# A decoder layer on one core: a long convolution done by halves of the channels, beside the projections

## The chip, the core and the metric

The kernel runs on one core of one Trainium2 chip, in float32. The core has a matrix engine (TensorE, PE in the profile), a vector engine (VectorE, DVE), a scalar engine (ScalarE, ACT), a general engine (GpSimd, POOL), a queue engine that issues DMAs (SyncE, SP), and 16 DMA engines which every queue shares. TensorE writes its products to PSUM, which has eight banks of 128 x 512 float32; the other data lies in SBUF, in 128 partitions, or in DRAM. The metric is the time on the device in microseconds (us), the median of several executions of the same program.

## What is computed

One decoder layer over 16 sequences of 512 tokens and 256 channels: a long-convolution block with a gated MLP, an attention block over the sequence and a context, and a low-rank feed-forward block, each followed by a layer norm of the sum. The change lies in the first block, whose mixing part is this:

```python
z = rmsnorm(u, pre_norm_w) @ in_proj_w.T            # 256 -> 768 channels
z_pre = depthwise_conv(z, short_w, 3 taps) + short_b
x2, x1, v = split(z_pre, 3)                         # 256 channels each
h = sum(residues[:, :, None] * exp(log_poles * t), axis=1)   # 256 filters, 512 long
xv = x1 * v
yconv = causal_conv(xv, h)                          # by rfft in the reference
y = (yconv + xv * D_skip) * x2
y = y @ out_proj_w.T + u
```

x2 is called the gate in the kernel.

## The kernel before

**A planner.** Nearly all work is recorded as operations with an engine (or two to choose from), a guessed cost, a priority number, the buffers it reads and writes, and a latency for DMAs. `Plan.schedule` (L104) plays the operations through with these costs: whenever an engine is free, it takes the startable operation with the lowest priority number. Buffers come from pools of a fixed number of tiles, and an operation is startable only when a tile is free. The result is a fixed order of instructions on each engine. On the chip each engine goes through its own list strictly in order and waits at an instruction until its inputs are there; the costs have no further effect. On TensorE, `change` (L96) adds `HOLD` or subtracts `STAY` to the priority, so that operations which split the array in the same way stay together. There are two plans, one for the front (L376, emitted at L875) and one for everything after it (L928, emitted at L1672). The second plan's instructions follow the first's on every engine.

**The front: projections.** For each sequence `project` (L422) loads x into a tile of the pool "x" (L428, after the preparation of the sequence three earlier), takes the sums of squares on ScalarE (L317), the power on GpSimd (L306 and L307), scales each of four chunks of rows on VectorE (L330), and transposes on TensorE (L344) with copies to a second "x" tile, xT. Six projections of 128 channels follow (L456, each into one bank of PSUM), with the short convolution on each: one tap and the bias on ScalarE (L463), two taps on VectorE straight from PSUM (L471). Projections 0 and 1 are the gate, which goes to DRAM (`gates`, L481). Projections 2 and 4, and 3 and 5, are multiplied on GpSimd (L487) to x1 * v of the first and the second 128 channels, transposed (L495) and copied into `xv` (L299 or L297 by engine), one tile of 256 channels x (4 pieces x 16 sequences) with the position in a piece along the partitions.

**The front: the long convolution.** Each channel's sequence of 512 is cut into 4 pieces of 128. Within a piece the convolution is a product with a 128 x 128 Toeplitz matrix, which is loaded from DRAM (`hpad`, L593, 0.5 MB for eight channels, in a tile of "x") and cut to a triangle on GpSimd (L602). Between pieces the filter is a sum of 16 exponentials, so that states are enough: `near_mm` (L619) makes the states of the pieces, VectorE (L629) and GpSimd (L639, L647) chain them, and `far_mm` (L683) multiplies them by powers of the poles, which ScalarE makes (L655). `toe_mm` (L670) and `far_mm` add up in the same PSUM bank; a copy (L299 or L297) takes it out, and two stores on ScalarE's queue (L701) write it to `yconv` in DRAM. There are eight blocks of 32 channels. Every block needs `xv` of all sequences: an operation there reads the whole of `xv`, and so all blocks stand behind the last sequence's projections.

**Pools and order.** Pool "x" has 11 tiles, used by x, xT, the Toeplitz tiles and `far`; "row" has nine of 128 x 512; "mm" is the eight banks of PSUM. Five Toeplitz loads are allowed early, the others after the last sequence's preparation (L595). The main stage begins with `first_block` (L996), which loads `yconv` (L1002, two halves), the gate (L1008) and x (L1011) for one sequence, multiplies on GpSimd (L1020) and projects on TensorE (L1033). The tiles of the main stage lie where the front's tiles lay and wait for those to be released. At its beginning it also fills some constant tiles and stores four small ones in DRAM (L924).

Of the kernel before, what the change touches and what calls it, by code (L numbers as in the profile page):

```python
# [61 lines left out]
class Plan:  # L62
# [9 lines left out]
    def __init__(self, tiles):  # L72
        self.tiles, self.ops = tiles, []

# [18 lines left out]

    HOLD, STAY = 1000, 1000
# [104 lines left out]
def decoder_layer(  # L199
# [71 lines left out]
    gates = dram.tile([B, P, KD * T], F32, name="gates")  # L271
    weights = ctx.enter_context(tc.tile_pool(name="weights", bufs=1))
# [52 lines left out]
    def scale_ops(x, sq, prio, on="DVE"):  # L325
        for c in range(NT):

            def fn(e, c=c):
                if e == "DVE":
                    nc.vector.tensor_scalar(x.t[:, c, :], x.t[:, c, :], sq.t[:, c, 8:9], None, ALU.mult)  # L330
                else:
                    nc.scalar.activation(x.t[:, c, :], x.t[:, c, :], AF.Copy, scale=sq.t[:, c, 8:9])

            plan.op(on, 0.4 if on == "DVE" else act(D, True), fn, prio, r=[sq], w=[(x, c)])
# [24 lines left out]

    R8 = 8  # L360
    NR = D // HPG
    with ExitStack() as front:
        fp_ = front.enter_context(tc.tile_pool(name="front", bufs=1))
        fps = front.enter_context(tc.tile_pool(name="psf", bufs=1, space=PSUM))
        pool = {
            "mm": tiles(fps, "fmm", 8, [P, T]),
            "x": tiles(fp_, "fx", 11, [P, R8 * P]),
# [8 lines left out]
        plan = Plan(pool)  # L376
# [4 lines left out]

        xv = fp_.tile([P, D, NT * B], F32, name="xv")
# [29 lines left out]
        XV, HPAD, NEAR, INW, CW, LP, W = (Buf("none") for _ in range(7))  # L412
        pool["none"] = [None] * 7
        marks = []

        def at_seq(b):
            return marks[b : b + 1] if b >= 0 else ()

        def load_in(dst, src, prio, w, after=()):
            plan.op("SP", 0.4, lambda e: nc.sync.dma_start(out=dst, in_=src), prio, w=w, lat=4.0, after=after)  # L420

        def project(b):  # L422

            pr = b * 100
            x_ = View("x", lambda t: t.rearrange("p (c d) -> p c d", c=NT))
            plan.op(
                "SP", 0.4,
                lambda e: nc.sync.dma_start(out=x_.t, in_=x[b].rearrange("(c p) d -> p c d", p=P)), pr - 1000,  # L428
                w=[x_], lat=4.0, after=at_seq(b - 3),
# [17 lines left out]
            scale_ops(x_, sq, pr - 120)  # L447
            xT = transposed(x_, lambda t: t, pr - 120, View("x", lambda t: t.rearrange("p (k n) -> p k n", k=KD)))
            marks.append(plan.ops[-1])
            zs = {}  # L450
            for m in (2, 4, 3, 5, 0, 1):
                ps, t = Buf("mm"), Buf("row")

                def mm(e, m=m, ps=ps):
                    for k in range(KD):
                        nc.tensor.matmul(  # L456
                            ps.t, inw[:, k, bass.ts(m, P)], xT.t[:, k, :], start=(k == 0), stop=(k == KD - 1)
                        )

                plan.op("PE", KD * pe(T), mm, pr + 10, r=[xT, INW], w=[ps])  # L460
                plan.op(
                    "ACT", act(T, True),
                    lambda e, m=m, ps=ps, t=t: nc.scalar.activation(  # L463
                        t.t, ps.t, AF.Identity, bias=cb[:, m : m + 1], scale=cw[:, m, 2:3]
                    ),
                    pr + 10, r=[ps, CW], w=[t],
                )
                for lag in (1, 2):
                    plan.op(
                        "DVE", dve(T) + 0.05,  # L470
                        lambda e, m=m, lag=lag, ps=ps, t=t: nc.vector.scalar_tensor_tensor(  # L471
                            t.t[:, lag:], ps.t[:, 0 : T - lag], cw[:, m, 2 - lag : 3 - lag], t.t[:, lag:],
                            ALU.mult, ALU.add,
                        ),
                        pr + 10, r=[ps], w=[t],
                    )
                zs[m] = t
                if m < KD:
                    plan.op(
                        "SP", 0.4,  # L480
                        lambda e, m=m, t=t: nc.sync.dma_start(out=gates[b][:, bass.ts(m, T)], in_=t.t), pr,  # L481
                        r=[t], lat=3.0,
                    )
            for k in range(KD):
                plan.op(
                    "POOL", 1.3,
                    lambda e, a=zs[KD + k], c=zs[2 * KD + k]: nc.gpsimd.tensor_tensor(a.t, a.t, c.t, ALU.mult),  # L487
                    pr, r=[zs[2 * KD + k]], w=[zs[KD + k]],
                )
            for k in range(KD):  # L490
                ps = Buf("mm")

                def tr(e, k=k, ps=ps):
                    for j in range(NT):
                        nc.tensor.transpose(ps.t[:, bass.ts(j, P)], zs[KD + k].t[:, bass.ts(j, P)], ident)  # L495

                plan.op("PE", TR, tr, pr, r=[zs[KD + k]], w=[ps])
                plan.op(
                    "ACT DVE", (1.04, 1.04),
                    lambda e, k=k, ps=ps: copy(  # L500
                        e, xv[:, bass.ts(k, P), b :: B].rearrange("p d j -> p j d"),
                        ps.t.rearrange("p (j d) -> p j d", j=NT),
                    ),
                    pr, r=[ps], w=[(XV, (b, k))],
                )

        for b in range(B):
            project(b)

        for k, (dst, src) in enumerate(((lp, poles), (rs, resid))):  # L510
            load_in(dst[:, :, 0:NS], src, 100 + k, [(LP, k)], at_seq(0))
        load_in(sk, skip, 102, [(LP, 2)], at_seq(0))
        load_in(lprow.rearrange("(k p) n -> p k n", p=P), poles, 110, [(NEAR, "row")], at_seq(1))
# [68 lines left out]
        for blk in range(NR // R8):  # L582
            pc = 5000 + blk * 100
            d0 = blk * R8 * HPG
            toes = []
            for c in range(HPG):
                toe = View("x", lambda t: t.rearrange("p (d u) -> p d u", u=P))

                def load_toe(e, toe=toe, at=d0 + c * R8):
# [5 lines left out]
                early = blk * HPG + c < 5  # L595
                plan.op(
                    "SP", 0.4, load_toe, pc - 50, r=[HPAD], w=[toe], lat=4.0,
                    after=at_seq(4 + c if early else B - 1),
# [13 lines left out]
            far = View("x", lambda t: t.rearrange("p (r u) -> p r u", u=P))  # L612
            for rr in range(0, R8, 2):

                def near_mm(e, rr=rr, ps=ps, d0=d0):
                    for r in range(rr, rr + 2):
                        for c in range(HPG):
                            d = d0 + c * R8 + r
                            nc.tensor.matmul(  # L619
                                ps.t[bass.ts(c, SLOT), bass.ts(r, (NT - 1) * B)],  # L620
                                near[:, d * NS : d * NS + SLOT], xv[:, d, 0 : (NT - 1) * B],
                                start=True, stop=True,
                            )

                plan.op("PE", 0.25, near_mm, pc, r=[XV, NEAR], w=[ps], tiling=COLS4)
# [370 lines left out]
    def first_block(b, after):  # L996
# [16 lines left out]
        for k in range(KD):  # L1013
            plan.op("SP", 0.1, lambda e, k=k: load_y(e, k), p0 - 500, w=[(yt, k)], lat=4.0)
# [740 lines left out]
```

## Time and profile before

| | us |
|---|---|
| median of 3 runs | 2184.96 |
| lowest and highest | 2181.42, 2185.18 |
| the profiled execution, its own time | 2186.31 |
| its span, first to last instruction | 2184.6 |
| TensorE busy in the span | 2037.0 (93%) |
| VectorE busy | 1361.0 (62%) |
| ScalarE busy | 943.6 (43%) |
| GpSimd busy | 663.5 (30%) |
| mean clock granted to TensorE | 0.97 of full speed |

The profile is one execution. Its span runs from the first to the last instruction; the execution's own time is 1.7 us longer. A line of groups reads: line of the kernel, engine, operation, tile written <- tiles read, shapes, count; then busy us and mean ns of one; then how long the engine stood idle just before such instructions and which instruction released it. PEld is TensorE's loading of weights, which overlaps its matmuls. A busy share over the whole span is a mean over stages with different limits, so the pieces of the span are read one by one. These are the page's own slices, 54.6 us each:

```profile
PE   8999758979899999999999999999999999999676
DVE  7988311746565757575757575757575757575642
PEclk9999978989999999999999999999999999999888
DMA  5342582122222222222232313131313131212200
```

The first six slices are the front.

### The profile page before, as it was taken

The numbers are of one execution on the slowest core, as the hardware profiler recorded it, in microseconds if no ns is written. First come the engines' busy times: TensorE is split into PE (matmuls) and PEld (weight loads), VectorE is DVE, ScalarE is ACT, GpSimd is POOL, SyncE is SP. The second block draws the span as 40 slices with busy tenths as digits, with TensorE's granted clock in tenths as the row PEclk, the third lists the DMA queues.
The fourth block names the chain that finished last, engine by engine and source line by source line (L and its number), as shares of the span: only waits on it lengthen the run. The fifth ranks groups of instructions, "written<-read, shape, count | busy, mean of one in ns | idle before, by whom it ended". The sixth has DMA issues, their size and how long they took to land.

```text
span 2184.6 us, 35354 instructions
## 1 busy us (share of the span) xinstructions
PE 2037.0 (93%) x14324; PEld 1053.6 (48%) x14324; DVE 1361.0 (62%) x1988; ACT 943.6 (43%) x1385; POOL 663.5 (30%) x896
## 2 busy tenths in 40 slices
PE   8999758979899999999999999999999999999676
PEld 4444545535454545454545454545454545454332
DVE  7988311746565757575757575757575757575642
ACT  7765312142526262626262626262626262625243
POOL 3333451131323232324232424242424242323222
PEclk9999978989999999999999999999999999999888
DMA  5342582122222222222232313131313131212200
GB/s 176 123 133 83 198 270 73 49 63 66 70 59 89 59 88 61 83 66 86 62 91 57 94 55 93 56 94 55 95 54 96 52 87 52 68 51 68 61 11 10
DMA packets 113733, 177.94 MB, mean 81 GB/s; under 512 B 13217, under 2 KB 61858, under 8 KB 113442
## 3 DMA queue, kind: packets, MB, share of 16 engines
q1 hardware_dynamic: 108450, 167.29, 25.0%
q10 hardware_dynamic: 5120, 8.39, 1.2%
q8 instruction: 112, 1.84, 0.3%
q14 instruction: 51, 0.42, 0.1%
HBM read 109.00 MB, written 66.67 MB: 80 GB/s over the span
## 4 chain that ended last, share of the span: by engine, by line
PE 84%; ACT 5%; DVE 5%; DMA 3%; issue 2%; POOL 1%; ACTq 0%; SPq 0%; POOLq 0%; DVEq 0%
PE mm L1058 13%; PE scores L1302 10%; PE mm L1211 8%; PE mm L1110 7%; PE scores L1380 7%; PE av L1415 7%; PE fmm L456 6%; PE mm L1605 4%; PE av L1621 3%; PE mm L1139 3%; PE mm L972 2%; DMA fx<-hpad 2%; PE mm L344 2%; PE mm L1467 2%; ACT ex L1392 2%
## 5 line engine op out<-in xcount | busy, mean ns | idle before, releaser
L1392 ACT ACTIVATE ex<-scores 128x2048 f32<-128x2048 f32 x160 | 300.1, 1876 | 176.7 <-PE scores L1380 174.0
L1058 PE MATMUL mm<-xT,w_l 128*128 128x512 f32 x640 | 296.0, 606 | 0.0
L1403 POOL TENSOR_SCALAR_AFFINE_SELECT ex<-ex 128x512 f32<-128x512 f32 x256 | 158.0, 635 | 382.4 <-ACT ex L1392 351.1
L1302 PE MATMUL scores<-keys,q 32*128 32x320 f32 (+4 forms) x2560 | 233.8, 472 | 42.8 <-DVE maxes L1332 18.3
L1321 DVE TENSOR_TENSOR scores<-scores,mask_qk 128x512 f32<-128x512 f32 (+1 forms) x192 | 168.3, 876 | 101.9 <-PE scores L1302 97.9
L1302 PEld LDWEIGHTS scores<-keys,q 32*128 32x128 f32 x2560 | 116.5, 190 | 179.0 <-issue 57.8
L1613 ACT ACTIVATE row<-mm,b_s 128x512 f32<-128x512 f32 x128 | 80.8, 684 | 253.6 <-PE mm L1605 253.4
L1380 PE MATMUL scores<-q,keys 32*128 32x512 f32 (+3 forms) x2048 | 183.1, 460 | 7.1 <-ACT ex L1392 7.0
L1058 PEld LDWEIGHTS mm<-xT,w_l 128*128 128x128 f32 x640 | 115.6, 190 | 145.9 <-issue 128.6
L456 PE MATMUL fmm<-fx,inw 128*128 128x512 f32 x384 | 177.2, 607 | 2.2 <-ACT fx L299 2.2
L957 ACT ACTIVATE xt<-xt,small 128x256 f32<-128x256 f32 x192 | 102.7, 595 | 173.7 <-POOL small L950 173.7
L1549 POOL TENSOR_TENSOR nd<-nd,nd 128x1024 f32<-128x1024 f32 x30 | 70.6, 2354 | 347.3 <-DMA nd<-di 347.3
L1415 PE MATMUL av<-ex,va 128*32 128x512 f32 (+3 forms) x2048 | 168.1, 439 | 0.0
L306 POOL TENSOR_SCALAR small<-small 128x4 f32<-128x4 f32 (+1 forms) x66 | 13.1, 199 | 509.6 <-DVE small L942 508.1
L1070 ACT ACTIVATE row<-mm 128x512 f32<-128x512 f32 x80 | 47.8, 597 | 271.0 <-PE mm L1058 271.0
L297 DVE COPY row<-av 128x512 f32<-128x512 f32 x66 | 45.7, 692 | 184.0 <-PE av L1415 165.5
L1110 PE MATMUL mm<-w_l,gT 128*128 128x256 f32 x640 | 158.9, 384 | 0.0
L471 DVE SCALAR_TENSOR_TENSOR frow<-fmm,cw,frow 128x511 f32<-128x511 f32 x192 | 140.2, 745 | 14.5 <-ACT frow L463 10.5
L1334 DVE TENSOR_REDUCE maxes<-scores 128x4 f32<-128x2048 f32 x64 | 146.7, 2293 | 2.2
L1380 PEld LDWEIGHTS scores<-q,keys 32*128 32x128 f32 x2048 | 89.3, 183 | 104.4 <-ACT ex L1392 33.8
L1110 PEld LDWEIGHTS mm<-w_l,gT 128*128 128x128 f32 x640 | 117.9, 190 | 43.8 <-issue 30.3
L1217 DVE TENSOR_SCALAR q<-mm,bqc_s 128x512 f32<-128x512 f32 x63 | 47.3, 751 | 140.0 <-PE mm L1211 140.0
(177 smaller groups left out, 3322.8 us busy)
## 6 DMA issues: line engine op xcount, KB each, us to landing
dn<-row SPq DMA_DIRECT2D x120, 256.0 KB
fx<-hpad SPq DMA_DIRECT2D x32, 512.0 KB
keys<-dk SPq DMA_DIRECT2D x64, 256.0 KB
nd<-dn SPq DMA_DIRECT2D x30, 512.0 KB
nd<-di SPq DMA_DIRECT2D x30, 512.0 KB
fx<-in_x SPq DMA_DIRECT2D x16, 512.0 KB
gates<-frow SPq DMA_DIRECT2D x32, 256.0 KB
yconv<-frow ACTq DMA_DIRECT2D x64, 128.0 KB
```

The source lines that it names most:

```text
L456: nc.tensor.matmul(ps.t, inw[:, k, bass.ts(m, P)], xT.t[:, k, :], start=(k == 0), stop=(k == KD - 1))
L471: lambda e, m=m, lag=lag, ps=ps, t=t: nc.vector.scalar_tensor_tensor(t.t[:, lag:], ps.t[:, 0 : T - lag], cw[:, m, 2 - lag : 3 - lag], t.t[ ...
L1058: nc.tensor.matmul(ps.t, w[:, k, bass.ts(f, P)], zT.t[:, k, :], start=(k == 0), stop=(k == KD - 1))
L1110: nc.tensor.matmul(ps.t[:, bass.ts(cc, D)], gT.t[:, f, bass.ts(c, P)] if f < NF else gE.t, w_l3[:, f, :] if f < NF else w_l3e[:, c, :], st ...
L1211: nc.tensor.matmul(ps.t, w[:, k, cols], xT.t[:, k, :], start=(k == 0), stop=(k == KD - 1))
L1302: nc.tensor.matmul(sc.t[:, r, at : at + hi - lo], q.t[hd, bass.ts(i, P)], kk.t[hd, lo:hi], start=True, stop=True,)
L1321: nc.vector.tensor_tensor(diag, diag, mask, ALU.add)
L1334: nc.vector.tensor_reduce(own[:, 3], sc.t, AX.X, ALU.max, negate=True)
L1380: nc.tensor.matmul(sc.t[:, r, at : at + T - j * P], keys[g].t[hd, TC + j * P : TC + (j + 1) * P], qas[g].t[hd, j * P :], start=True, stop= ...
L1392: lambda e, sc=sc, ex=ex: nc.scalar.activation(ex.t.rearrange("p (r n) -> p r n", r=HPG), sc.t, AF.Exp, scale=scale),
L1403: lambda e, ex=ex, at=at: nc.gpsimd.affine_select(out=ex.t.rearrange("p (r n) -> p r n", r=HPG)[:, :, at : at + P], in_=ex.t.rearrange("p ...
L1415: nc.tensor.matmul(av[g].t[bass.ts(r, SLOT), j * P :], va.t[:, j, h * VS : h * VS + SLOT], ex.t[:, r * T + at : r * T + at + n], start=(j ...
```

## The change

The convolution is done by halves of the channels. `xv` becomes two tiles, one for each 128 channels, with a dependency of its own, so that the first four blocks need only the first half of x1 * v. The loop over sequences is split: `prepare` makes xT, `x1v(b, k, ...)` makes one half of x1 * v for a sequence, `gate_of` makes its gate. The first seven sequences do all of it as before. The last nine (`LATE`) do only the first half of x1 * v in this pass; their second halves and gates follow with higher priority numbers (3000 and up), between the operations of the first half's convolution (2000 to 2310). The last two gates (`LAST`) have 7000, behind the second half's convolution (5400 and up). The xT of the last five sequences (`KEPT`) stays in its tile until then. Four others are written to a new array in DRAM, `normed`, and read back.

Beside that:

- The scaling of rows in the front moves from VectorE to GpSimd (`scale_ops(..., "POOL")`).
- The `yconv` stores move from ScalarE's queue to SP, with a planned cost of 0.6.
- `far` gets a tile of its own, one, and "x" has 10 tiles in place of 11.
- `near_mm` of a block is one operation in place of four, `far_mm` one in place of two, with its two halves of the array taken in turn.
- A projection holds its "row" tile from the matmul on, and near_mm its "state" tile.
- The planned costs of DMAs on SP follow their size (`MB` = 3.5 us for 1 MB), and the planned latencies are changed.
- In the front's plan `HOLD` is 0 in place of 1000. The main plan keeps 1000 and 1000.
- In `first_block` x and the gate are loaded ahead of `yconv`, with a planned cost of 0.5 in place of 0.1.
- Three Toeplitz loads are allowed early, after the preparations 13 to 15; the second half's after the second-half x1 * v of the sixth late sequence.

The diff, cut to its core:

```diff
-                if e == "DVE":
-                    nc.vector.tensor_scalar(x.t[:, c, :], x.t[:, c, :], sq.t[:, c, 8:9], None, ALU.mult)
+                if e == "POOL":
+                    nc.gpsimd.tensor_scalar(x.t[:, c, :], x.t[:, c, :], sq.t[:, c, 8:9], None, ALU.mult)
...
+        xv = [fp_.tile([P, P, NT * B], F32, name=f"xv{k}") for k in range(KD)]
...
-            "x": tiles(fp_, "fx", 11, [P, R8 * P]),
+            "x": tiles(fp_, "fx", 10, [P, R8 * P]),
+            "far": tiles(fp_, "far", 1, [P, R8, P]),
...
-        plan = Plan(pool)
+        plan = Plan(pool, 0, 1000)
...
-        xv = fp_.tile([P, D, NT * B], F32, name="xv")
...
+        LATE, KEPT, LAST = 9, 5, 2
...
+        def x1v(b, k, xT, pr):
+
+            a, c = project(KD + k, xT, pr), project(2 * KD + k, xT, pr)
+            plan.op(
+                "POOL", 1.3, lambda e: nc.gpsimd.tensor_tensor(a.t, a.t, c.t, ALU.mult), pr, r=[c], w=[a]
+            )
+            ps = Buf("mm")
...
+            plan.op("PE", TR, tr, pr, r=[a], w=[ps])
+            plan.op(
+                "ACT DVE", (1.04, 1.04),
+                lambda e: copy(
+                    e, xv[k][:, :, b::B].rearrange("p d j -> p j d"), ps.t.rearrange("p (j d) -> p j d", j=NT)
+                ),
+                pr, r=[ps], w=[(XV[k], b)],
+            )
+
+        def gate_of(b, xT, pr):
+            for m in range(KD):
+                t = project(m, xT, pr)
+                plan.op(
+                    "SP", 0.25 * MB,
+                    lambda e, m=m, t=t: nc.sync.dma_start(out=gates[b][:, bass.ts(m, T)], in_=t.t), pr,
+                    r=[t], lat=2.5,
+                )
+
+        late, late_T = [], []
+        for b in range(B):
+            xT = prepare(b, b * 100)
+            x1v(b, 0, xT, b * 100)
+            if b < B - LATE:
+                x1v(b, 1, xT, b * 100)
+                gate_of(b, xT, b * 100)
+            else:
+                if b < B - KEPT:
+                    plan.op(
+                        "SP", 0.5 * MB,
+                        lambda e, b=b, xT=xT: nc.sync.dma_start(
+                            out=normed[b - B + LATE], in_=xT.t.rearrange("p k n -> p (k n)")
+                        ),
+                        b * 100 + 20, r=[xT], w=[(NORMED, b)], lat=2.5,
+                    )
+                late.append((b, xT))
+        for b, xT in late:
+            if b < B - KEPT:
+                xT = as_xT()
+                plan.op(
+                    "SP", 0.5 * MB,
+                    lambda e, b=b, xT=xT: nc.sync.dma_start(
+                        out=xT.t.rearrange("p k n -> p (k n)"), in_=normed[b - B + LATE]
+                    ),
+                    1900 + b, r=[(NORMED, b)], w=[xT], lat=2.5, after=at_step(B - 1 - 2 * (b % 2)),
+                )
+            late_T.append((b, xT))
+            x1v(b, 1, xT, 3000 + b * 100)
+            marks.append(plan.ops[-1])
+            if b < B - LAST:
+                gate_of(b, xT, 3000 + b * 100)
+        for b, xT in late_T[LATE - LAST :]:
+            gate_of(b, xT, 7000 + b * 100)
...
-            pc = 5000 + blk * 100
             d0 = blk * R8 * HPG
+            kh, x0 = d0 // P, d0 % P
+            pc = (5000 if kh else 2000) + blk * 100
...
-                early = blk * HPG + c < 5
+                n = blk * HPG + c
                 plan.op(
-                    "SP", 0.4, load_toe, pc - 50, r=[HPAD], w=[toe], lat=4.0,
-                    after=at_seq(4 + c if early else B - 1),
+                    "SP", 0.5 * MB, load_toe, pc - 50, r=[HPAD], w=[toe], lat=2.5,
+                    after=at_step(B - 3 + n if n < 3 else B - 1 if not kh else B + LATE - 4),
                 )
...
-            far = View("x", lambda t: t.rearrange("p (r u) -> p r u", u=P))
-            for rr in range(0, R8, 2):
+            far = Buf("far")
+            def near_mm(e, ps=ps, d0=d0, kh=kh, x0=x0):
+                for r in range(R8):
...
+            plan.op("PE", 1.0, near_mm, pc, r=[XV[kh], NEAR], w=[ps], tiling=COLS4, holds=[st])
...
                 for par in range(2):
                     plan.op(
-                        "ACT", 0.1,
-                        lambda e, c=c, o=o, par=par, d0=d0: nc.scalar.dma_start(
+                        "SP", 0.6,
+                        lambda e, c=c, o=o, par=par, d0=d0: nc.sync.dma_start(
...
+        plan.op("SP", 0.5, load_x, p0 - 500, w=[x_], lat=4.0)
+        plan.op("SP", 0.5, load_g, p0 - 500, w=[gate], lat=4.0)
         for k in range(KD):
-            plan.op("SP", 0.1, lambda e, k=k: load_y(e, k), p0 - 500, w=[(yt, k)], lat=4.0)
-        plan.op("SP", 0.1, load_g, p0 - 500, w=[gate], lat=4.0)
-        plan.op("SP", 0.1, load_x, p0 - 500, w=[x_], lat=4.0)
+            plan.op("SP", 0.5, lambda e, k=k: load_y(e, k), p0 - 500, w=[(yt, k)], lat=4.0)
```

## The prediction

> **What bounds the kernel now.** I first read the slices of the page, then cut the span at the instants where the kind of work changes, and asked for the busy time of each engine in each piece. The columns are busy us and number of instructions for each engine, the clock granted to TensorE, the share of the DMA engines and their rate.
>
> ```profile
> 0.00:229.00 229.00, 207.29 (x684) 104.65 (x684) 196.00 (x338) 151.19 (x337) 81.55 (x102) 0.98 0.40 127
> 229.00:309.00 80.00, 56.99 (x1537) 51.61 (x1536) 14.59 (x26) 18.88 (x48) 43.61 (x62) 0.87 0.75 260
> 309.00:326.00 17.00, 0.00 (x0) 0.00 (x0) 2.70 (x4) 1.26 (x3) 4.04 (x10) 0.50 0.75 208
> 326.00:2184.60 1858.60, 1772.75 (x12104) 897.35 (x12104) 1147.69 (x1622) 772.28 (x999) 534.35 (x724) 0.98 0.23 67
> ```
>
> The front is the first 326 us. While it projects (0 to 229) TensorE is busy 207.3 us and VectorE 196.0: both nearly full. While it convolves (229 to 309) TensorE is busy 57.0 of 80 us, VectorE 14.6, and the DMA engines carry 260 GB/s: data-bound, with VectorE and ScalarE almost idle. From 309 to 326 TensorE does nothing. Everything after is one long TensorE-bound stage. So two stages with different limits stand one after the other, and the gap between them is where an overlap can gain. Second view, the groups of the projecting stage (line, engine, operation, out<-in, count | busy us, mean ns | idle before):
>
> ```profile
> L456 PE MATMUL fmm<-fx,inw 128*128 128x512 f32 x384 | 177.2, 607 | 2.2 <-ACT fx L299 2.2
> L471 DVE SCALAR_TENSOR_TENSOR frow<-fmm,cw,frow 128x511 f32<-128x511 f32 (+1 forms) x190 | 138.7, 745 | 14.4 <-ACT frow L463 10.5
> L487 POOL TENSOR_TENSOR frow<-frow,frow 128x512 f32<-128x512 f32 x32 | 40.7, 1273 | 93.9 <-DVE frow L471 54.8 <-ACT frow L463 37.5 <-PE fmm L344 1.6
> L330 DVE TENSOR_SCALAR fx<-fx,fsmall 128x256 f32<-128x256 f32 x63 | 20.2, 374 | 1.6 <-POOL fsmall L307 1.6
> L307 POOL TENSOR_TENSOR fsmall<-fsmall,mhalf 128x4 f32<-128x4 f32 x15 | 15.4, 1028 | 1.3
> L787 POOL TENSOR_SCALAR w_l<-w_l,postw 128x672 f32<-128x672 f32 x4 | 7.9, 1998 | 1.8 <-DMA postw<-in_post_w 1.8
> ```
>
> L330 is what the change moves to GpSimd, which is idle for most of this stage. Third, the order of time at the seam (start, us, engine, line):
>
> ```profile
> 314.17 0.58 ACT L299 COPY frow<-fmm 128x512 f32<-128x512 f32 x1 [1.17 <-issue]
> 314.25 3.79 ACTq L701 DMA_DIRECT2D yconv<-frow  x6
> 315.46 5.55 SPq L1002 DMA_DIRECT2D yt<-yconv  x2
> ...
> 321.06 0.50 SPq L1008 DMA_DIRECT2D gate<-gates  x1
> ...
> 325.06 2.49 POOL L1020 TENSOR_TENSOR yt<-yt,gate 128x512 f32<-128x512 f32 x2 [3.06 <-DMA gate<-gates]
> ```
>
> The last matmul of the front ends at 308.5; copies on ScalarE stand between DMA issues of the same queue, the last result is stored at 320.6, and then the gate is fetched behind it. The next matmul starts at 326.4, after 17.9 us. In the chain of waits "PE fmm L456" has 6% and "DMA fx<-hpad" 2% of the whole span, which is the same picture.
>
> **The change part by part.** Matmuls: none is added or removed, so TensorE's work up to the seam stays 207.3 + 57.0 = 264.3 us. In the changed order of instructions the first-half convolution (4 of 8 blocks) stands among the projections: its first near product is row 138 of TensorE, the second half's first is row 320, and projections stand between most of its pieces. The order of TensorE, VectorE, ScalarE and GpSimd from the first block on is the old one, so I leave the 1858.6 us after 326 as they are; on SP some loads there change places, and those waited for nothing that ends last.
>
> (1) Start. The first sequence's rows are scaled on GpSimd. The trace has no such tile there. Below: a copy of 128x256 (L737) takes 0.42 us. Above: a product of 128x512 (L487), 1.27. Nearest is the same operation at 128x672 (L787), 1.998; with 0.210 for 128x4 (L306) a straight line gives 0.88 at 256. I take 0.85, 3.4 us for four, against 1.14 us for four on VectorE at 8.96. First matmuls 9.4 + 2.3 = 11.7 us. At the ends 0.42 and 1.27 it would be 9.9 and 13.3.
>
> (2) Projections, 207.3 us of TensorE as before, and the first half of the convolution, half of 57.0, 28.5 us, now in the same stretch.
>
> (3) Idle of TensorE in that stretch. Before, 229 - 9.4 - 207.3 = 12.3 us. VectorE loses L330 (20.2 us) and gains half of the state products and copies (some 8 us), so it goes from 196 busy us in 229 to about 187 in 257: waits for it shrink. Against that, new waits in the convolution: with ten tiles, five of them kept, five turn over for 16 Toeplitz loads; per load an issue of 0.5 us, 4.5 to 7 us to land (4.46 to 7.68 in the chain), 1.09 for the select (L602), and stores of the block before stand ahead on SP (8 x 0.55 us). Between such a load and its matmul the new order has mostly 6 to 9 us of projections, so most are covered; if that cover were gone each of 16 loads would cost up to those 7 us. DMA: 16 loads of 0.52 MB, 4.2 MB of stores, four xT written and read back (4.2 MB) and 14 gates of 0.26 MB make 20.5 MB in about 80 us, 256 GB/s, under the 318 to 340 that 250 to 300 reached. I take 9 us of idle, between 0 and 25. The first stretch ends at 11.7 + 207.3 + 28.5 + 9 = 256.5.
>
> (4) GpSimd in the thin part. From the eighth sequence on, a first pass has two projections, not six. Over the last eight preparations the new order holds 62 us of TensorE (1.72 a projection, 0.44 a group of transposes) and on GpSimd 8 x (4 x 0.85 + 1.26) + 14 x 1.27 + 8.0 = 63 us. Level at 0.85, so charged within the 9 us; at 1.27 it is 76 us, 14 more; at 0.42 GpSimd has 13 us to spare.
>
> A page speaks against this move. The row first: on VectorE, L557 (two inputs in SBUF) at 20.69 took 1.27 us while L487 ran on GpSimd from 20.54 to 21.81; at 23.32, with GpSimd idle, 0.34. L471, one input of which is in PSUM, took its usual 0.75 under L487.
>
> ```profile
> 20.54 1.27 POOL L487 TENSOR_TENSOR frow<-frow,frow 128x512 f32<-128x512 f32 x1 [5.64 <-ACT frow L463]
> 20.69 1.27 DVE L557 SCALAR_TENSOR_TENSOR h<-e,rs,h 128x128 f32<-128x128 f32 x1
> 23.32 0.34 DVE L557 SCALAR_TENSOR_TENSOR h<-e,rs,h 128x128 f32<-128x128 f32 x1
> ```
>
> The Trainium skill, page "Perfetto Trace Analysis", section "Optimizing Scalar/DVE Operations", says that GpSimd and VectorE share a read port, so moving work between the two might not help. By it the saving on VectorE would be nothing and the forecast's idle would stay 12 us, 3 us later. The row agrees only for L557 and its like; L471 is the bulk.
>
> By the rows alone, 64 scalings of 0.85 us can hold up 30 L557 by at most 0.85 each, 25 us of VectorE, in the first 70 us, where VectorE has (196.0 - 20.2) / 16 = 11.0 us a sequence to TensorE's 13.0: inside the 0 to 25.
>
> (5) Second half. It needs 28.5 us of TensorE. By the order, eight of its 16 Toeplitz loads are released about 20 us before the projections end, 4.2 MB at 260 GB/s being 16 us; the others follow as tiles come free, the last behind the eight stores of its first block. There is now a single far tile, so two blocks' far products are at least 8 x 0.39 (L655) + 1.6 = 4.7 us apart, hidden beside 6.8 us of other products a block. I take 30 us, between 28 and 40 (half of the old 80).
>
> (6) Seam. After the last far product: two copies an engine 1.3 us, eight stores on SP at 0.55, 4.4, landing 3.15, the load of the second half of yt 3.9 with its issue 0.5, product 1.27: 14.5, and four small stores to dk stand ahead of that load, 2.5 us of issue, mostly under the landing. I take 15, between 13 and 19 (it was 17.9). The gate and the first half of yt are fetched earlier, so nothing else waits there.
>
> Sum: 256.5 + 30 + 15 = 301.5 against 326.4, a gain of 24.9 us. The profiled execution took 2186.3 us with a span of 2184.6, and lies 1.3 us over the median 2184.96. 2184.96 - 24.9 = **2160 us**.
>
> **The rivals.** *GpSimd and turnover take the gain* (the scaling costs 1.27, or the five tiles turn slower): 14 us of (4) or 25 for 9 of (3), about 15 us less gain: 2175. For it: GpSimd is level with TensorE in (4) and instructions stand in a fixed order on each queue. Against: the same rows give slack at 0.85. *TensorE runs dense*: priced by the dense stretches of the chain (96 x 1.72 + 64 x 0.44 + 4, 198 us) projections need 9 us less than 207.3, idle falls to 5 and the second half to 28: 15 us more gain, 2145. For it: VectorE's relief. Against: 0.93 and 0.86 of granted clock in slices of the old stage. *Slower*: SP becomes a ring. Stores that used to stand on ScalarE's queue now stand ahead of the next loads. If nothing covered it a block would need 1.3 + 4.4 + 6.9 (load) + 1.1 + 0.95 + 1.6 = 16.3 us, 130 for eight, with projections standing behind in TensorE's order: 11.7 + 207.3 + 12 + 130 + 15 = 376, 50 us later: 2235. It decides from 25 us of waits, 3.1 a block, on. Against it: projections between the pieces, and ten tiles in the second half. *No overlap at all* is excluded by the order of instructions, which shows the near product of half one ahead of 26 projections (45 us of TensorE).
>
> **How the numbers follow.** Forecast 0.52 (2160), GpSimd and turnover 0.22 (2175), dense 0.18 (2145), ring 0.08 (2190 to 2235). The forecast's own range is 2152 to 2170. The range, 2143 to 2179, takes in the two neighbours. 0.2%, 4.4 us, is about what this measurement tells from no change: faster 0.87, same 0.05, slower 0.08 (the ring; the same is the upper end of the second case).
>
> **What would show it.** The first matmul of the main stage near 301 instead of 326; TensorE busy over 90% up to 256; L330 on GpSimd near 0.85 us; VectorE's waits for GpSimd absent; DMA rate in the middle of the front near 250 GB/s; the main stage 1858 us. I am wrong if TensorE waits for Toeplitz tiles among the projections by more than 25 us, if the scaling takes over 1.2 us, or if the main stage itself changes.

## The result and the profile after

The changed kernel takes 2162.18 us, the median of 4 runs (2160.58 to 2162.7); the kernel before 2183.36 us, the median of the three runs of its table and one more (2181.42 to 2185.18). The ratio is 0.9902, with a 95% interval of 0.9885 to 0.9919: 21 us less. The forecast was 2160 in 2143 to 2179. The profiled execution took 2162.7 us with a span of 2161.0.

First view: the span of the changed kernel cut where the kind of work changes, with the columns of the prediction's pieces (us; busy us and instructions of TensorE, weight loads, VectorE, ScalarE, GpSimd; granted clock; DMA share; GB/s).

```profile
0.00:249.80 249.80, 230.18 (x1452) 124.23 (x1452) 183.97 (x290) 157.41 (x349) 164.59 (x200) 0.99 0.60 190
249.80:280.00 30.20, 25.11 (x769) 22.34 (x768) 7.87 (x14) 11.15 (x32) 15.38 (x24) 0.94 0.74 220
280.00:304.70 24.70, 2.08 (x4) 1.17 (x4) 2.58 (x4) 0.92 (x2) 7.78 (x14) 0.52 0.78 215
304.70:2161.00 1856.30, 1770.91 (x12100) 896.17 (x12100) 1147.69 (x1622) 772.29 (x999) 532.88 (x722) 0.98 0.22 66
```

The three pieces of the front, 229 + 80 + 17, have become 249.8 + 30.2 + 24.7: TensorE is now busy 92% of a first stretch that holds half of the convolution, the convolution left over is 50 us shorter, and the empty seam is longer than it was. The main stage is what it was: 1856.3 us, and the four products (2.08 us) that it was counted with before now lie in the seam.

Second view: groups of the front (lines of the changed kernel; L469, L716, L728, L665, L484, L330 and L496 were L456, L670, L683, L619, L471, L330 and L487).

```profile
L469 PE MATMUL fmm<-fx,inw 128*128 128x512 f32 x384 | 176.8, 605 | 0.0
...
L716 PE MATMUL fmm<-fx,xv 128*64 128x128 f32 x512 | 33.1, 284 | 2.5 <-issue 2.3 <-POOL fx L650 0.2
L728 PE MATMUL fmm<-far,state 16*64 16x128 f32 x512 | 10.2, 280 | 1.2 <-ACT far L701 1.2
L665 PE MATMUL fmm<-xv,near 128*32 128x48 f32 x512 | 7.0, 207 | 3.1 <-issue 1.6 <-ACT frow L299 1.4
...
L330 POOL TENSOR_SCALAR fx<-fx,fsmall 128x256 f32<-128x256 f32 x64 | 58.2, 924 | 1.4
L496 POOL TENSOR_TENSOR frow<-frow,frow 128x512 f32<-128x512 f32 x32 | 40.7, 1274 | 47.1 <-DVE frow L484 36.8 <-ACT frow L476 7.5 <-ACT xv L299 1.6
...
L484 DVE SCALAR_TENSOR_TENSOR frow<-fmm,cw,frow 128x511 f32<-128x511 f32 x192 | 140.6, 744 | 36.8 <-ACT frow L476 32.6 <-DMA gates<-frow 0.2
```

The same three convolution groups in the kernel before:

```profile
L670 PE MATMUL fmm<-fx,xv 128*64 128x128 f32 x512 | 37.2, 307 | 15.6 <-POOL tmp L639 6.5 <-POOL fx L602 6.0 <-issue 2.4
...
L683 PE MATMUL fmm<-fx,state 16*64 16x128 f32 x512 | 13.0, 274 | 0.5 <-POOL state L647 0.5
L619 PE MATMUL fmm<-xv,near 128*32 128x48 f32 x512 | 7.7, 225 | 6.3 <-issue 6.3
```

Two gains can be read here. TensorE's idle time in front of these groups fell from 22.4 us (15.6 + 0.5 + 6.3) to 6.8 (2.5 + 1.2 + 3.1): the waits for cut Toeplitz tiles (L602, now L650) from 6.0 to 0.2, those for the chained states (L639 and L647) from 7.0 to none. And the same 1536 matmuls were busy 50.3 us (33.1 + 10.2 + 7.0) instead of 57.9; the granted clock is 0.99 and 0.94 in the two pieces, in place of 0.87. How much of either is owed to the overlap is the first experiment's question.

Third view: the order of time in the seam (start, us, engine, line), from the last store of `yconv` to the second half of the first output product.

```profile
288.21 0.59 SPq L746 DMA_DIRECT2D yconv<-frow  x1
288.85 0.59 SPq L1056 DMA_DIRECT2D xt<-in_x  x1
289.45 2.05 POOL L958 MEMSET va<- 128x1152 f32 x2 [13.65 <-DMA yconv<-frow]
289.48 0.55 SPq L1053 DMA_DIRECT2D gate<-gates  x1
290.07 0.43 SPq L1047 DMA_DIRECT2D yt<-yconv  x1
...
292.76 1.49 DVE L967 TENSOR_SCALAR row<-row,one 128x512 f32<-128x512 f32 x2 [11.66 <-POOL row L966]
293.16 1.55 POOL L971 MEMSET maxes<- 128x512 f32 x2
293.53 2.99 SPq L969 DMA_DIRECT2D dk<-row  x4
295.76 1.26 POOL L1065 TENSOR_TENSOR yt<-yt,gate 128x512 f32<-128x512 f32 x1 [1.05 <-DMA yt<-yconv]
296.56 1.33 SPq L1047 DMA_DIRECT2D yt<-yconv  x1
...
303.43 1.26 POOL L1065 TENSOR_TENSOR yt<-yt,gate 128x512 f32<-128x512 f32 x1 [6.41 <-DMA yt<-yconv]
304.72 0.34 SPq L1053 DMA_DIRECT2D gate<-gates  x1
304.74 0.50 PEld L1078 LDWEIGHTS mm<-outw,yt 128*128 128x128 f32 x2 [6.32 <-POOL yt L1065]
```

The last matmul of the front ends at 279.8. The first half of yt is asked for at 290.07, the second only at 296.56: between them SP stands at the four constant stores of L969 (2.9 us of wait and 3.0 of issue). These wait for L967, that for GpSimd's constant tiles, and these for late `yconv` stores to land (the main stage's tiles lie where the front's lay). In the kernel before both halves of yt were asked for at 315.46, and the four stores stood behind them:

```profile
322.09 2.49 SPq L924 DMA_DIRECT2D dk<-row  x4
```

### The profile page after: what moved, and what is told of

The parts are those of the page before. It is cut to its first block, busy times and chain, and to the rows that moved or that the text cites. A ratio compares the mean times of both kernels' runs of the same rounds, so it can differ in the third digit from the quotient of the medians.

```text
span 2161.0 us, 35414 instructions
## 1 busy us (share of the span) xinstructions
PE 2028.3 (94%) x14324; PEld 1043.9 (48%) x14324; DVE 1342.1 (62%) x1928; ACT 941.8 (44%) x1381; POOL 720.6 (33%) x960
## 4 chain that ended last, share of the span: by engine, by line
PE 80%; ACT 5%; DVE 4%; issue 2%; POOL 2%; DMA 1%; SPq 0%; ACTq 0%; POOLq 0%; DVEq 0%
PE mm L1103 13%; PE scores L1347 10%; PE mm L1256 8%; PE mm L1155 8%; PE scores L1425 7%; PE av L1460 7%; PE mm L1650 4%; PE av L1666 3%; PE mm L1184 3%; PE mm L1017 2%; PE fmm L469 2%; PE mm L344 2%; PE mm L1512 2%; ACT ex L1437 2%; PE scores L1486 2%
## 5 line engine op out<-in xcount | busy, mean ns | idle before, releaser
L1347 PEld LDWEIGHTS scores<-keys,q 32*128 32x128 f32 x2560 | 116.5, 191 | 179.0 <-issue 57.9
L469 PE MATMUL fmm<-fx,inw 128*128 128x512 f32 x384 | 176.8, 605 | 0.0
L484 DVE SCALAR_TENSOR_TENSOR frow<-fmm,cw,frow 128x511 f32<-128x511 f32 x192 | 140.6, 744 | 36.8 <-ACT frow L476 32.6
L297 DVE COPY row<-av 128x512 f32<-128x512 f32 x66 | 45.7, 692 | 184.0 <-PE av L1460 165.5
## 6 DMA issues: line engine op xcount, KB each, us to landing
dn<-row SPq DMA_DIRECT2D x120, 256.0 KB
keys<-dk SPq DMA_DIRECT2D x64, 256.0 KB
gates<-frow SPq DMA_DIRECT2D x32, 256.0 KB
```

Of the source, the lines that this page charges most:

```text
L469: nc.tensor.matmul(ps.t, inw[:, k, bass.ts(m, P)], xT.t[:, k, :], start=(k == 0), stop=(k == KD - 1))
L484: lambda e, lag=lag: nc.vector.scalar_tensor_tensor(t.t[:, lag:], ps.t[:, 0 : T - lag], cw[:, m, 2 - lag : 3 - lag], t.t[:, lag:], ALU.mul ...
L1347: nc.tensor.matmul(sc.t[:, r, at : at + hi - lo], q.t[hd, bass.ts(i, P)], kk.t[hd, lo:hi], start=True, stop=True,)
```

## The experiments

**What is the overlap worth, all else as changed?** No sequence is late, and the Toeplitz loads go after the last preparation.

```diff
-        LATE, KEPT, LAST = 9, 5, 2
+        LATE, KEPT, LAST = 0, 0, 0
...
-                    after=at_step(B - 3 + n if n < 3 else B - 1 if not kh else B + LATE - 4),
+                    after=at_step(B - 3 + n if n < 3 else B - 1),
```

> The changed kernel with LATE, KEPT and LAST at 0: every sequence is finished in the first pass, so no projections are left beside the first half's convolution; scaling on GpSimd, stores on SP, two xv tiles and the far tile stay. If the gain is the overlap, TensorE first works through all projections (to about 9.6 + 207 + 10 = 227 us), then convolves for 60 to 80 us with the DMA engines near 250 to 300 GB/s, and the main stage starts near 325: 2178 to 2192 us. If the gain came from the edits beside the overlap (VectorE relieved, stores on SP, another order of loads), it stays within 6 us of 2162.

Measured: 2178.95 us, ratio to the kernel before 0.9972 (0.9961 to 0.9983); the profiled execution is this kernel's fastest (2175.33). So the overlap itself is worth 17 us by the medians, 15 by the two ratios (0.9972 and 0.9902). TensorE's waits in the front, first of this kernel (engine and line, what it waited for: us in total, times, longest), then of the changed one:

```profile
PE fmm L716 <- POOL fx L650: 19.1, 6, 5.8
```

```profile
PE fmm L716 <- POOL fx L650: 0.2, 1, 0.2
```

L650 cuts a Toeplitz tile that has just landed. Where these 19.1 us stand, the pieces of this kernel show: up to the last far product of the first half, and the second half.

```profile
0.00:247.17 247.17, 226.39 (x1516) 124.89 (x1516) 182.42 (x285) 157.95 (x348) 157.14 (x195) 0.99 0.48 154
247.17:296.16 48.99, 29.57 (x704) 25.20 (x704) 6.76 (x11) 13.61 (x40) 23.15 (x30) 0.76 0.79 252
```

The first piece holds the work of the changed kernel's first 249.8 us, without projections beside the convolution, and is 2.6 us shorter. All of the 19.1 us stand in the second half, which takes 49.0 us instead of 30.0. The seam is 3.8 us shorter (21.1 instead of 24.9). So 19.0 - 2.6 - 3.8 = 12.6 us, the difference of the two profiled spans. SP's order of time in the second half, first of this kernel, then of the changed one:

```profile
251.24 4.96 SPq L746 DMA_DIRECT2D yconv<-frow  x8
256.29 4.60 SPq L641 DMA_DIRECT2D fx<-hpad  x7
...
275.06 4.97 SPq L746 DMA_DIRECT2D yconv<-frow  x8
280.13 4.51 SPq L641 DMA_DIRECT2D fx<-hpad  x6
```

```profile
253.45 3.81 SPq L641 DMA_DIRECT2D fx<-hpad  x5
261.33 5.82 SPq L746 DMA_DIRECT2D yconv<-frow  x8
267.25 1.04 SPq L641 DMA_DIRECT2D fx<-hpad  x1
```

In this kernel all 16 Toeplitz loads of the second half are issued right behind a run of eight `yconv` stores. SP's own waits from 236 to 296 say what held them: 14.9 us for the results that the stores carry (L297 and L299) and 1.1 us at the loads themselves, so tiles were free by then and the stores ahead held the loads, by these waits and by about 5 to 7 us of issue for each run. In the changed kernel 9 of the 16 go out between 230.96 and 246.4, while TensorE still projects, and 15 before that half's own first run of stores, at 261.33 (with none late 9, before 268.04). So what the late projections cover is the loading of the second half's tiles; in the first half this kernel does not wait for tiles either.

The price of the matmuls follows the waits. In this one run the 256 Toeplitz products (L716) of the first half are busy 15.4 us at a granted clock of 0.99, those of the second half 21.8 at 0.76. The 1536 matmuls take 55.9 us here, between 57.9 before and 50.3 after: 2.0 us come with the change's other edits, 5.6 with the overlap. In TensorE's whole sum this does not show (256.0 us here, 255.3 in the changed kernel, whose projections were busier in its profile), so the difference of these two profiles is idle time.

**Is it the number of projections that covers them?** Five late sequences in place of nine.

```diff
-        LATE, KEPT, LAST = 9, 5, 2
+        LATE, KEPT, LAST = 5, 5, 2
```

> The changed kernel with five late sequences instead of nine, so 16 projections fewer stand beside the first half's convolution (27 us of TensorE at 1.72 us each), and no xT goes through DRAM. Theory (the gain of the overlap is the cover that projections give to Toeplitz loads): between none late (2179) and nine (2162), at about 2168 to 2171, with more waits of TensorE for L650. Rival (the first projections suffice, nine is more than needed): 2160 to 2163.

Measured: 2174.14 us, 0.9952 (0.9937 to 0.9967). The waits in the whole front, then those of the second half alone, then that half in the columns of the first view:

```profile
PE fmm L716 <- POOL fx L650: 15.5, 4, 6.7
```

```profile
PE fmm L716 <- POOL fx L650: 14.3, 3, 6.7
```

```profile
244.50:294.08 49.58, 30.73 (x769) 27.51 (x768) 7.68 (x13) 11.00 (x31) 20.53 (x29) 0.73 0.68 209
```

The time lies between, about 5 us under none late, and the two intervals overlap a little. The expected figure was too low by 3 to 6 us, and its reason does not hold: among the projections TensorE waits only 1.2 us for tiles, with half as many of them beside the convolution. The other 14.3 us stand in the second half, which takes 49.6 us, as with none late. Here 10 of its 16 loads go out before its first run of stores (257.47); the other six follow by twos, each pair right behind such a run (264.17, 271.21, 282.14). So what goes with the time in these three kernels is how many of the second half's loads get ahead of its own stores on SP (9 with none late, 10 and 15), not waits among the projections. Whether another order on SP would do with five what nine do was not tried.

**What is the scaling on GpSimd worth?** Undone in the changed kernel, and then done alone in the kernel before.

```diff
-            scale_ops(x_, sq, pr - 120, "POOL")
+            scale_ops(x_, sq, pr - 120, "DVE")
```

> The changed kernel with the front's row scaling back on VectorE (planned cost 0.4, as before the change). If TensorE sets the stretch, VectorE goes from 184 to about 204 busy us in 250 and GpSimd from 165 to 110; the chain through GpSimd from 137 to 161 us goes away: 2154 to 2168 us. If the relief of VectorE is what lets the overlap run, TensorE waits for VectorE's taps again: 2172 us or more.

```diff
-            scale_ops(x_, sq, pr - 120)
+            scale_ops(x_, sq, pr - 120, "POOL")
```

> The kernel before with the scaling alone moved to GpSimd. If VectorE did not set the projecting stage, the convolution behind it stands unchanged and the time is 2178 to 2190 us. If the relief of VectorE (20 us of 196) is a part of the gain by itself, projections end some 8 us earlier: 2175 us or less.

Measured: undone in the changed kernel 2162.6 us, 0.9897 (0.988 to 0.9915), the same as with it; alone in the kernel before 2177.98 us, 0.9964 (0.9951 to 0.9977), some 6 us faster. The first stretches of the two, in the columns of the first view:

```profile
0.00:249.28 249.28, 227.12 (x1453) 121.62 (x1453) 207.64 (x353) 157.15 (x350) 106.99 (x136) 1.00 0.59 190
```

```profile
0.00:224.67 224.67, 204.62 (x684) 104.07 (x685) 175.23 (x271) 151.24 (x340) 138.52 (x166) 0.98 0.41 130
```

In the changed kernel VectorE has 207.6 us of work in 249 with the scaling and 184.0 without, and the stretch ends at the same instant: TensorE sets it. In the kernel before the stretch ended at 229.0 with VectorE at 196.0 and ends at 224.7 with 175.2. Of these 4.3 us 2.7 are TensorE's busy time and 1.7 its idle time, so that VectorE's relief is the cause of the gain is not shown; the time lies between the two expectations. The edit is a gain alone and nothing beside the overlap, so the parts of the change do not add up. The kernel with none late has this edit and all others but the overlap, and at 2178.95 us it is no faster than this edit alone.

**Are the stores on SP part of it?** The `yconv` stores go back to ScalarE's queue.

```diff
-                        "SP", 0.6,
-                        lambda e, c=c, o=o, par=par, d0=d0: nc.sync.dma_start(
+                        "ACT", 0.1,
+                        lambda e, c=c, o=o, par=par, d0=d0: nc.scalar.dma_start(
```

> The changed kernel with the yconv stores back on ScalarE's queue. If stores on SP are needed so that ScalarE can take the projections out of PSUM, the 32 stores of the first half now stand among 36 of those copies, each with 0.55 us and its waits: 2167 to 2185 us. If the ring on SP (stores ahead of the Toeplitz loads) was the dearer of the two, and the run of 16 stores at the seam, the time falls below 2158 us.

Measured: 2183.79 us, 0.9999 (0.9989 to 1.001): the whole gain is gone. The order of time on ScalarE in the overlapped stretch of this kernel:

```profile
187.33 0.59 ACT L299 COPY frow<-fmm 128x512 f32<-128x512 f32 x1 [2.85 <-PE fmm L728]
187.94 1.14 ACTq L746 DMA_DIRECT2D yconv<-frow  x2
189.18 0.58 ACT L299 COPY frow<-fmm 128x512 f32<-128x512 f32 x1 [1.26 <-PE fmm L665]
189.26 7.45 ACTq L746 DMA_DIRECT2D yconv<-frow  x6
196.75 2.45 ACT L701 ACTIVATE far<-ramp,lpT 128x128 f32<-128x128 f32 x8 [6.99 <-DMA yconv<-frow]
```

The powers of the poles for the next block (L701) stand behind eight stores: 7 us in which ScalarE computes nothing, though the copies that they store ended by 189.8; a single issue takes up to 1.5 us there. The changed kernel makes them at 188.03, right after the copies. VectorE's next taps, at 199.89, have then waited 10.1 us for ScalarE. The first stretch ends at 261.6 instead of 249.8: TensorE is busy 3.3 us longer in it and waits 4.4 us more for the products of GpSimd (L496), 4.3 more for L650 and 1.3 for L701. The second half takes 41 us instead of 30, and there it waits for L701 itself (1.2 us in the changed kernel):

```profile
PE fmm L728 <- ACT far L701: 9.4, 5, 6.5
```

The seam is 1 us shorter: 12 + 11 - 1 = 22 us, and the medians differ by 21.6. The planner put L701 behind the stores at a planned cost of 0.1 each; whether an order with L701 ahead of them would keep the gain was not tried. The Trainium skill, page "DMA: Bandwidth & Descriptors", section "Issuing engines are not separate DMA queues", says that issuing from several engines at once saves only the time of issue, which is usually small. Here an issue took 0.56 us at the median, and the run shows what else the choice of engine sets: who stands behind the issue.

**Do the constant stores make the seam long?** They go to ScalarE's queue, which has little to do there (0.92 us in the seam).

```diff
-            nc.sync.dma_start(out=t[bass.ts(par, HPG), HD:, :], in_=fixed[0 : HPG * HD, :])
+            nc.scalar.dma_start(out=t[bass.ts(par, HPG), HD:, :], in_=fixed[0 : HPG * HD, :])
```

> The changed kernel with the four constant stores of L969 on ScalarE's queue. Theory A (the seam of the changed kernel is 24.9 us and not 15 partly because the last yt transfer stands on SP's queue behind these four stores, which wait until 293.5): the last yt transfer is issued right after the first, near 290.7 instead of 296.6, the first output product at about 291 to 293 and the second half of them at about 299, and the time falls by 5 to 6 us, to about 2156. Rival B (the transfers themselves, 220 GB/s of other traffic, end where they end whatever the issue time): the last yt transfer still lands near 303 and the time stays at 2162 within 1 us.

Measured: 2154.51 us, 0.9856 (0.9841 to 0.987), 7.7 us under the changed kernel by the medians, 10 by the two ratios, and more than expected. The order of time:

```profile
286.75 2.06 POOL L958 MEMSET va<- 128x1152 f32 x2 [12.93 <-DMA yconv<-frow]
286.79 0.55 SPq L1053 DMA_DIRECT2D gate<-gates  x1
287.38 0.98 SPq L1047 DMA_DIRECT2D yt<-yconv  x2
...
291.76 3.04 ACTq L969 DMA_DIRECT2D dk<-row  x4
293.00 2.48 POOL L1065 TENSOR_TENSOR yt<-yt,gate 128x512 f32<-128x512 f32 x2 [1.55 <-DMA yt<-yconv]
```

Both halves of yt are asked for at 287.38 and land together; the last matmul of the front ends at 279.1 and the first product begins at 294.3, 15.3 us later, and nothing waits between its halves. The first product was expected earlier, at 291 to 293, and a wait for its second half, to 299, that is not there.

**Is it the run of stores?** Every second store of the last two blocks goes to ScalarE's queue, without and with the edit above.

```diff
-                        "SP", 0.6,
+                        "ACT" if par and blk >= 6 else "SP", 0.6,
```

> The changed kernel with every second yconv store of the last two blocks issued by ScalarE instead of SP. Theory A (the run of 16 stores on SP's queue, 0.62 us each, 278.6 to 288.8, holds the yt transfers back): the run ends some 4 to 5 us earlier; but the last yt transfer still stands behind the four constant stores that wait until about 293, so alone this is worth 0 to 3 us: 2159 to 2162. Rival B (stores on ScalarE's queue block ScalarE, as with all of them there): 2164 to 2170.

> Both edits of the last two blocks' stores and of the constant stores together. Theory A: the two waits on SP's queue add up, 5 to 6 us for the constant stores and 4 to 5 us for the halved run of stores: 2150 to 2154, first output product near 287. Rival B (traffic of the other loads sets when yt lands): 2160 to 2163.

Measured: 2161.87 us, 0.989 (0.9873 to 0.9906), alone; 2154.9 us, 0.9857 (0.9842 to 0.9872), with the constant stores moved. Shorter runs of stores bring nothing: the last far products end at 282.5 instead of 279.8, and at 281.1 instead of 279.1 with the constant stores moved, again because their powers (L701) stand behind stores on ScalarE, and that takes back what the queue gives.

**Two more tries at the seam**, both with the constant stores on ScalarE's queue: four stores of the last block alone on that queue (`"ACT" if par and blk == 7 else "SP"`), and in `first_block` the gate and yt loaded ahead of x; then both.

> The kernel with the constant stores on ScalarE's queue, and beside that four of the last block's eight yconv stores issued by ScalarE. Theory (the seam after the constant stores are gone is the chain of the last block: copies, the stores' issue, landing, the yt transfer; earlier blocks' stores on ScalarE cost 2 us because the last far powers stand behind them, and here they don't): about 2.5 us of issue less, 2152, first output product near 292 instead of 294.3. Rival (the DMA engines set when yt lands): 2154.5 within 1 us.

> The kernel with the constant stores on ScalarE's queue, and in the main stage's first block the gate and yt loaded ahead of x. Theory of order (on SP's queue each issue of 0.6 us ahead of yt holds it back): yt is issued 0.6 us earlier, and 0.5 MB of x no longer shares the DMA engines with it (2 us at 240 GB/s): 1 to 2.5 us less, 2152 to 2153.5. Rival (x then comes late for the sum after the product, 0.69 us at L1028, which needs it): 2155 to 2158.

> Both of these edits. If issue on SP's queue is what holds yt, they add up: 2150 to 2151. If the DMA engines' rate is, the first is worth nothing and this equals the kernel with x behind yt.

Measured: 2155.25 us (0.985 to 0.9884), 2155.4 us (0.985 to 0.9879) and 2154.46 us (0.9845 to 0.9874). None differs from 2154.51. From the last matmul of the front to the first product it is 15.1, 15.4 and 15.0 us. This stretch of the first of them, in the columns of the first view:

```profile
278.60:293.75 15.15, 0.04 (x5) 0.00 (x1) 3.94 (x5) 0.58 (x1) 6.02 (x14) 0.55 0.96 275
```

The DMA engines are busy 96% there. That agrees with the rival, that their rate sets when yt lands. Against its simple form, the second try took the 0.5 MB of x from ahead of yt, and yt was not ready sooner; other transfers were not moved, so this is not settled.

**Does GpSimd hold up the thin part?** The scaling of w_l (four instructions of 1.96 us at 140 us) goes behind the preparations.

```diff
-                    900, r=[W],
+                    2600, r=[W],
```

> The changed kernel with GpSimd's scaling of w_l (4 x 1.95 us at 140 us) planned after the preparations instead of before the last of them. Theory (GpSimd is full from 137 to 161 but TensorE is too, so TensorE sets the end of the first stretch): 2162 within 2 us. Rival (GpSimd's scaling at 0.92 us a tile is what paces the thin part): up to 7.8 us less, 2155.

Measured: 2164.1 us, 0.9899 (0.9884 to 0.9913): no change. GpSimd is full around 140 to 160 us, and that costs nothing.

## Why the prediction was right, step by step

- **The sum.** It put the start of the main stage's product at 301.5 us; the product's first half began at 297.1, the second, from which on the main stage runs, at 304.7. That 2160 and 2162.18 are so close is in part luck, since two terms were wrong with opposite signs: the first stretch ended 6.7 us earlier than forecast, the seam took 9.7 us longer.
- **(1) Start**, 11.7: measured 9.6. I let the first transpose wait for all four chunks; each waits for its own (L330, 0.92 us a chunk), and the rest of the lag shows as gaps between transposes.
- **(2) TensorE's work**, 207.3 + 28.5 = 235.8: measured 230.2. The step took busy time over from a stretch with a granted clock of 0.87. In the first stretch, at 0.99, half of the convolution takes 24.7 us, not 28.5; about 1 us of that is not the clock but the other edits (2.0 us for both halves, by the kernel with none late). The projections took 205.5 instead of 207.3, and no run shows why. The Trainium skill, page "TensorE: Matmul & The Clock Gate", section "HAM oscillation — how this bites in real kernels", describes the mechanism, a clock that falls when pauses for data recur; the rows agree (307 ns a matmul of L670 at 0.87, 284 ns of L716 as a whole; 15.4 and 21.8 us for the two halves of L716 in the kernel with none late, at 0.99 and 0.76).
- **(3) Idle**, 9: measured 249.8 - 9.6 - 230.2 = 10.0. Waits for Toeplitz tiles are 0.2 of it. That it takes projections between the pieces to cover them is not confirmed: with none late the first half does not wait for tiles either.
- **(4) Scaling**, 0.85 us: measured 0.92. Level with TensorE in the thin part, and without effect, as charged. The weighed rule of a shared port did not decide: L484, which reads PSUM, stayed at 744 ns beside a GpSimd that was busy 165 us of the stretch, the two-input L557, now L604, took 400 ns on the mean after 419, and alone in the kernel before the move did help. What failed is a silent assumption, that VectorE's relief is part of the gain: undone, the time is the same.
- **(5) Second half**, 30: measured 30.2, and for the stated reason: nine of its 16 loads go out from 230.96 on, 19 us before the projections end. With none late it takes 49.0. This is where most of the overlap's gain lies.
- **(6) Seam**, 15 (13 to 19): measured 24.7. This is the mis-sized term. I saw the four constant stores ahead of the second half of yt, and priced them at 2.5 us of issue, "mostly under the landing". But they wait themselves, for constant tiles that wait for late `yconv` stores to land: SP stands until 293.5, and their issue takes 3.0 us more. With them out of the queue it is 15.3, and the time 2154.5.
- **The rivals.** *GpSimd and turnover*: the scaling costs 0.92, not 1.27, and the tiles turn in time. *TensorE dense*: half true, TensorE's work in the front fell by 9 us (264.3 to 255.3), its idle time not below the forecast. *Ring*: real, but avoided here: loads behind stores on SP cost TensorE 19.1 us of waits with none late, 14.3 with five, and 0.2 in the changed kernel; putting the stores back costs more, 21.6 us. Taking the main stage over unchanged was right.

No version is faster, beyond the noise, than the changed kernel with the constant stores on ScalarE's queue: 2154.51 us, 0.9856 of the kernel before.

## What to carry to other kernels

A small store in an in-order queue costs its issue and, on top, what its inputs make it wait: follow each instruction that stands ahead of a critical load back to its own inputs. The same holds for loads behind stores of results: look for the time in which the next stage's loads can go out ahead of them, and let other work fill it. When work moves from a stage with pauses into a dense one, price it at the clock of the new stage. And test the parts of a change alone and undone: here one part was worth 6 us alone and nothing beside the others, and another, the place of the stores, cost the whole gain when it was undone.

## What the runs showed of the hardware

- The issue of one 128 KB store held ScalarE for 0.45 to 1.53 us while the DMA engines were loaded, six in a row for 7.45 us; on SP sixteen took 10 to 11 us.
- The same 256 matmuls (L716, 128x128) were busy 15.4 us in a stretch with a granted clock of 0.99 and 21.8 us in one with waits and 0.76, in one run.
- A multiplication of 128x256 by a column took 0.92 us on GpSimd (58.2 us for 64) and 0.37 us on VectorE in the kernel before; in the changed kernel it took VectorE 0.47 (27.0 us for 64 there: more, but with no effect on the time).
